# A state-space scan over both channel tiles in one instruction, and no tap products on TensorE

## The chip, the cores and the metric

The kernel runs on one core of a Trainium2 chip. The metric is the device time of one execution in microseconds, the median of several runs. A profile of one execution stands beside it; its own time is given where it is used. The names of the engines are those of the profile: PE is TensorE (PEld its weight loads), DVE is VectorE, ACT is ScalarE, POOL is GpSimd and SP is SyncE.

## The reference

Eight images of 256 channels and 1024 positions pass through a state-space block with an MLP, then through attention and a mixture of experts. The change concerns the state-space block alone:

```python
xz = x @ W_in
xm, z = jnp.split(xz, 2, axis=-1)                # 512 channels each
xp = jnp.pad(xm, ((0, 0), (d_conv - 1, 0), (0, 0)))
xm = sum((xp[:, k:k + L, :] * conv_w[:, k] for k in range(d_conv))) + conv_b   # 4 taps
xm = jax.nn.silu(xm)
dbl = xm @ W_x
dt, Bm, Cm = jnp.split(dbl, [dt_rank, dt_rank + d_state], axis=-1)
dt = jax.nn.softplus(dt @ W_dt + b_dt)
A = -jnp.exp(A_log)

def step(h, inputs):                             # 1024 positions, 16 states a channel
    dt_t, B_t, C_t, x_t = inputs
    dA = jnp.exp(dt_t[..., None] * A)
    h = dA * h + (dt_t * x_t)[..., None] * B_t[:, None, :]
    y = jnp.einsum('bds,bs->bd', h, C_t)
    return (h, y)

y = ys.transpose(1, 0, 2) + xm * D_param
y = y * jax.nn.silu(z)
return y @ W_out
```

For each image, channel and state, `h` is a linear recurrence over the positions: a decay `dA`, an input, and a sum over states of `h` times `C`.

## The kernel before, in words

The work is cut into 16 chunks `i` of 512 positions (`CH`), two for each image; `c = i % NCH` is 0 for an image's first chunk and 1 for its second. The 512 channels lie in four tiles of 128 partitions; two tiles make a half `h`. A chunk has 32 steps (`NSTEP`): 16 states times two halves, numbered on through all chunks as `g`. A step handles one state `s` for one half, that is [128, 2, 512] numbers.

The main loop (L2226 on) writes the steps out one after the other. For step `now` it issues:

- `scan`: the recurrence, on DVE, in place in a tile `hb`. In an image's first chunk the two channel tiles lie one behind the other as 1024 columns and one scan runs over both, because the decay of the second tile's first column is zero and no state is carried in. In the second chunk each channel tile has a scan of its own that begins from its column of `state`. In the first chunk POOL then copies the last column of both tiles to `state`.
- `decay` of step `now + 2`: the exponentials that make `da_all`, on ACT, in one of two buffers. In second chunks the one for the first tile is issued between the two scans.
- `inputs` of step `now + 1`: the product of `xd` with the broadcast row of B, on DVE, into a free `hb`.
- `sums` of `now`: the product with the row of C, on DVE, in place in `hb`; then a DMA issued by POOL adds `hb` to the accumulator `acc` (named `dx` in the profile), which began as D times x. Two accumulators are in use, one for each half, so each such DMA follows the one of two steps before.

`hb` has four slots (`h4`); a fifth is the tile of the weights `w_z`, once they are no longer needed (it appears in the profile as `w_z`). The tiles `t4` (25) hold everything else of this size.

Everything else runs as generators ("streams") beside this loop: `prologue` (projection, the four taps, softplus, for the next chunk), `epilogue` (gate, output projection, MLP), `attention`, `project`, `experts`. `advance()` steps them as long as a small planner, which adds up an estimated cost for each engine, says that their engine is due. The order on each engine's queue is thus fixed when the program is built, and each engine works through its queue in that order. `FRONT[i]` is the step of chunk `i` at which the next chunk's prologue starts, `GATE[i]` that of its gate. `SOFT[i]` lets POOL's DMAs and ACT do two products of the softplus that DVE does otherwise.

The four taps are, as a rule, one ACT operation and three DVE multiply-adds for each channel tile (`conv_parked`, L635; `conv_dve` for the first two chunks). Where `CONV[i]` is 1 (chunks 3, 4 and 13) they are products on PE with diagonal blocks `taps`, 64 matrix products a chunk, which the profile counts as 128:

```python
for r in range(4):
    rows = slice(HD * r, HD * r + HD)
    pe.matmul(
        ps[rows, :], taps[rows, d * KW + t, :], xps[q][rows, t : t + CH],
        start=(t == 0), stop=(t == KW - 1),
    )
```

POOL's queue holds the state copies, all accumulating DMAs (those of the steps; those of softplus into `dt`; those of the epilogue, the projection and the experts' results) and the gathers of expert weights (`g<-eW_d,rows`, `g<-in_eW,rows`), six at a time.

Of the kernel before, what the change touches and what calls it, by code (L numbers as in the profile page):

```python
# [54 lines left out]
def hybrid_kernel(ctx: ExitStack, tc: tile.TileContext, a: dict, out: bass.AP):  # L55
# [95 lines left out]
    w_z = load("w_z", [P, KC, DI], a["W_in"].rearrange("(k p) n -> p k n", p=P)[:, :, DI:])  # L151
# [69 lines left out]
    taps = const.tile([P, ND * KW, HD], F32, name="taps")  # L221
# [50 lines left out]
    FRONT = (7, 13, 4, 4, 1, 14, 10, 1, 13, 1, 10, 6, 1, 5, 10)  # L272
    GATE = (20, 4, 30, 30, 22, 7, 30, 18, 28, 25, 5, 28, 30, 30, 12, 26)
    CONV = (0, 0, 0, 1, 1, 0, 0, 0, 0, 0, 0, 0, 0, 1, 0, 0)
    SOFT = (1, 0, 0, 1, 0, 0, 0, 0, 1, 0, 1, 0, 0, 0, 0, 0)
# [274 lines left out]
    set_up, gates_ready, centered_w = [], [], []  # L550
# [43 lines left out]
    def conv_pe(i, xn, mem):  # L594


        c = i % NCH
        while not set_up:
            yield POLL
        xm, xp, ps, ps2 = [], None, None, None  # L600
        for d in range(ND + 1):
            if d < ND:
                if d % 2 == 0:
                    xm.append((yield from mem.take(f"xm_{i}_{d // 2}")))

                ps2 = yield from banks.take(f"xin_{i}_{d}")
                for k in range(KC):
                    pe.matmul(
                        ps2, w_in[:, k, d * P : (d + 1) * P], xn[:, k, :],
                        start=(k == 0), stop=(k == KC - 1),  # L610
                    )
            if d:
                for t in range(KW):
                    for r in range(4):
                        rows = slice(HD * r, HD * r + HD)
                        pe.matmul(
                            ps[rows, :], taps[rows, (d - 1) * KW + t, :], xp[rows, t : t + CH],
                            start=(t == 0), stop=(t == KW - 1),
                        )
                if c < NCH - 1:  # L620
                    act.copy(conv_tail[:, c + 1, d - 1, :], xp[:, CH:])
            yield
            if d:
                h, q = divmod(d - 1, 2)
                act.activation(xm[h][:, q, :], ps, AF.Identity, bias=V("conv_b", d - 1))
                banks.put(ps)
            if d < ND:
                xp = work_pool.tile([P, KW - 1 + CH], F32, name=f"xp_{i}_{d}", tag="xp", bufs=2)
                act.activation(xp[:, KW - 1 :], ps2, AF.Identity, bias=b_in[:, d : d + 1])
                act.copy(xp[:, : KW - 1], conv_tail[:, c, d, :])  # L630
                ps = ps2
            yield
        return xm

    def conv_parked(i, mem):  # L635
# [5 lines left out]
        for h in range(NHALF):  # L641
# [11 lines left out]
            if CONV[i]:  # L653
                for q in range(2):
                    d = 2 * h + q
                    ps = yield from banks.take(f"cv_{i}_{d}")
                    for t in range(KW):
                        for r in range(4):
                            rows = slice(HD * r, HD * r + HD)
                            pe.matmul(  # L660
                                ps[rows, :], taps[rows, d * KW + t, :], xps[q][rows, t : t + CH],
                                start=(t == 0), stop=(t == KW - 1),
                            )
                    yield
                    act.activation(xm[h][:, q, :], ps, AF.Identity, bias=V("conv_b", d))
                    banks.put(ps)
                continue
# [17 lines left out]
    def prologue(i: int):  # L685
# [23 lines left out]
        def skip_path():  # L709

            for h in range(NHALF):
                dx = me["acc", h] = yield from mem.take(f"dx_{i}_{h}")
                for r in range(2):
                    act.activation(
                        dx[:, r, :], xm[h][:, r, :], AF.Identity, scale=V("D", 2 * h + r)
                    )
# [160 lines left out]

    def load_bc(n):
# [12 lines left out]
    def decay(g, q):  # L891
        i, s, h = place(g)
        da = da_all[:, g % 2, q, :]
# [4 lines left out]
        if skip and g % NSTEP < 2:  # L898
            act.copy(da[:, :1], zero_c)
# [8 lines left out]
    def inputs(g):  # L908
# [11 lines left out]
    def scan(g, q):  # L920

        i, s, h = place(g)
        c = i % NCH
        hb = hbs[g]
        d = 2 * h + q
        done = das.pop((g, q))
        vec.at = max(vec.at, done)
        if c == 0:
            if q:
                both = hb.rearrange("p a t -> p (a t)")  # L930
                vec.tensor_tensor_scan(
                    both, da_all[:, g % 2].rearrange("p a t -> p (a t)"), both, 0.0,
                    ALU.mult, ALU.add,
                )
        else:
            vec.tensor_tensor_scan(
                hb[:, q, :], da_all[:, g % 2, q, :], hb[:, q, :], state[:, s, d : d + 1],
                ALU.mult, ALU.add,
            )
        if q and c < NCH - 1:  # L940
            pool.tensor_copy(state[:, s, 2 * h : 2 * h + 2], hb[:, :, CH - 1])

    def sums(g):
# [14 lines left out]
    def park():  # L958
# [29 lines left out]
        h4.make = lambda nm, k: w_z if k == H4 else make(nm, k)  # L988
# [50 lines left out]
    def epilogue(i: int):  # L1039
# [20 lines left out]
        for h in range(NHALF):  # L1060
            yield me["landed", h]
            if c < NCH - 1:
                vec.tensor_tensor(
                    me["acc", h][:, :, CH - 1], me["dx_end"][:, 0, h], me["dx_end"][:, 1, h],
                    ALU.add,
                )
            vec.tensor_tensor(y[h], me["acc", h], y[h], ALU.mult)
# [1008 lines left out]
    with tc.tile_pool(name="work", bufs=1) as work_pool:  # L2076

        def tagged(tag, n):
            return Slots(
                lambda nm, k: work_pool.tile([P, 2, CH], F32, name=nm, tag=f"{tag}_{k}"), n  # L2080
            )
# [81 lines left out]
        def setup():  # L2163
# [15 lines left out]
            blk = pl.tmp("eye_b", [P, HD], F32)  # L2179
            yield  # L2180
            for r in range(4):
                rows = slice(HD * r, HD * r + HD)
                vec.tensor_copy(blk[rows, :], eye[rows, rows])
            vec.tensor_tensor(
                taps, blk.unsqueeze(1).to_broadcast([P, ND * KW, HD]),
                V("conv_w").unsqueeze(2).to_broadcast([P, ND * KW, HD]), ALU.mult,
# [358 lines left out]
```

## Time and profile before

| | before |
|---|---|
| median of 3 runs | 3393.05 us (3391.55 to 3400.25) |
| the profiled execution's own time | 3395.24 us |
| its span | 3393.4 us |
| mean granted TensorE clock | 0.963 |
| scans of 512 columns (second chunks) | 448 + 64 at 1268 and 1266 ns |
| scans of 1024 columns (first chunks) | 225 + 31 at 2285 and 2282 ns |
| products with B, with C | 512 each, about 1.20 and 1.22 us |
| exponentials of a step's decays, ACT | two, about 0.72 us each |
| state copies, POOL | 225 + 31, 0.18 to 5.5 us, median 1.03 us |
| accumulating DMAs of the steps | 449 + 63, issue 0.89 to 0.94 us, median landing after 7.8 and 6.7 us |
| tap products on PE | 384, 43.4 us busy |
| multiply-adds of the taps, DVE | 156, 741 ns |
| gathers of expert weights, POOL | 64 at 1563 ns and 32 at 1424 ns |

The span is the time from the first to the last instruction of the program; the execution's own time has some 2 us around it. Where two counts are given, the second is that of the slot that bears the name `w_z`. In the tables of stretches each line has the stretch, its length, and for PE, PEld, DVE, ACT and POOL the busy time with the number of instructions, then the granted clock, the DMA engines' busy share, and GB/s. In the views by order of time a line has start, duration, engine, line, operation, output and inputs, shape, and in brackets the idle time before it and what ended it. Nearly all lines of code are L98 or L95, since one helper records every instruction.

### The profile page before, as it was taken

What the parts mean: (1) busy time and instruction counts of PE and PEld (TensorE: products, weight loads), DVE (VectorE), ACT (ScalarE), POOL (GpSimd) and SP (SyncE); (2) the same over time, 40 slices, a digit from 0 to 9 for tenths busy, and PEclk for the clock granted to TensorE, in tenths of its full rate; (3) what the DMA queues carried; (4) which work ended last, traced back from release to release, by engine and by line L of the source; (5) the groups of instructions that cost most, each with busy time, mean ns of one, the idle gap of its engine ahead of it and who ended that gap; (6) DMA issues with size and microseconds to landing.
All of it is one profiled execution on the core that took longest, in us unless ns stands there. A gap on an engine that the chain in (4) does not pass through costs nothing. (4 is left out here: it accounts for less than half of the span.)

```text
span 3393.4 us, 44585 instructions
## 1 busy us (share of the span) xinstructions
PE 3141.3 (93%) x16359; PEld 1387.0 (41%) x16359; DVE 2993.7 (88%) x3140; ACT 2467.8 (73%) x3610; POOL 1104.5 (33%) x1072
## 2 busy tenths in 40 slices
PE   8888988999899999999999899999899989999998
PEld 5444443433343334333444344333443343334343
DVE  6999999899999979899999999999999999962561
ACT  4766756678867887687779777787768868864643
POOL 0242145313432235334353245133542453211010
PEclk9989989999999999999999999999999989999999
DMA  4877899989988898889998999799998998972140
GB/s 138 237 204 189 218 219 219 227 209 232 222 218 228 195 214 202 211 206 217 225 250 190 224 228 216 185 217 219 232 237 201 227 224 186 211 171 71 39 96 23
DMA packets 216134, 668.21 MB, mean 197 GB/s; under 512 B 31200, under 2 KB 42592, under 8 KB 215904
## 3 DMA queue, kind: packets, MB, share of 16 engines
q0 software_dynamic: 106112, 373.88, 56.5%
q1 hardware_dynamic: 109792, 291.38, 25.3%
q8 instruction: 130, 2.13, 0.2%
q14 instruction: 100, 0.82, 0.1%
HBM read 269.20 MB, written 92.93 MB: 107 GB/s over the span
## 5 line engine op out<-in xcount | busy, mean ns | idle before, releaser
L98 ACT ACTIVATE da_all<-dt,vecs 128x512 f32<-128x512 f32 (+1 forms) x1024 | 699.4, 717 | 287.9 <-DVE hb L98 244.8
L95 POOL DMA_DIRECT2D dx<-hb x449 | 397.3, 890 | 1363.5 <-DVE hb L98 960.8
L98 DVE TENSOR_TENSOR hb<-xm,bc 128x1024 f32<-128x1024 f32 x449 | 540.0, 1203 | 22.5 <-issue 19.8
L98 DVE TENSOR_TENSOR_SCAN hb<-da_all,state,hb 128x512 f32<-128x512 f32 x448 | 552.7, 1268 | 4.2 <-ACT da_all L98 4.1
L98 ACT ACTIVATE pt<-sc 128x1024 f32<-128x1024 f32 x512 | 494.6, 1018 | 81.5 <-PE sc L98 70.9
L98 DVE TENSOR_TENSOR hb<-hb,bc 128x1022 f32<-128x1022 f32 (+1 forms) x449 | 546.7, 1218 | 0.0
L98 DVE TENSOR_TENSOR_SCAN hb<-da_all,hb 128x1024 f32<-128x1024 f32 x225 | 514.2, 2285 | 8.3 <-ACT da_all L98 8.3
L98 PE MATMUL warm<-mean_c,zero_c 128*128 128x256 f32 x1182 | 366.0, 433 | 48.9 <-ACT z L98 11.5
L98 POOL COPY state<-hb 128x2 f32<-128x2 f32 x225 | 330.6, 1471 | 206.4 <-DVE hb L98 201.2
L98 PE MATMUL sc<-qk,qk 32*128 32x512 f32 x2048 | 337.7, 647 | 18.2 <-ACT pt L98 17.1
L98 PEld LDWEIGHTS warm<-mean_c,zero_c 128*128 128x128 f32 x1182 | 219.6, 206 | 191.7 <-PE warm L98 73.3
L98 PE MATMUL num<-pt,v 128*32 128x512 f32 x2048 | 279.6, 616 | 13.2 <-DVE ot L98 13.2
L98 PE MATMUL den<-pt,ecb 128*32 128x512 f32 x1792 | 239.0, 604 | 0.0
L98 PE MATMUL re<-he,g 128*128 128x512 f32 x472 | 221.6, 615 | 18.5 <-ACT sz L98 7.8
L98 PE MATMUL facc<-fh,w 128*128 128x512 f32 x512 | 232.8, 601 | 5.9 <-ACT fo L98 2.4
L98 PE MATMUL fh<-x_f,w 128*128 128x512 f32 x480 | 227.1, 604 | 7.2 <-DVE x_f L98 2.5
L98 PE MATMUL he<-xe,g 128*128 128x512 f32 x448 | 219.0, 615 | 5.7 <-issue 3.5
L98 ACT ACT_TABLE_LOAD x159 | 204.0, 1283 | 3.5 <-PEq L2532 0.7
L98 PEld LDWEIGHTS sc<-qk,qk 32*128 32x128 f32 x2048 | 101.0, 185 | 198.3 <-ACT pt L98 80.3
L98 PEld LDWEIGHTS facc<-fh,w 128*128 128x128 f32 x512 | 95.4, 192 | 132.3 <-issue 118.1
L98 PEld LDWEIGHTS re<-he,g 128*128 128x128 f32 x472 | 89.9, 196 | 133.2 <-issue 103.8
L98 PEld LDWEIGHTS fh<-x_f,w 128*128 128x128 f32 x480 | 86.5, 190 | 133.9 <-issue 100.3
(422 smaller groups left out, 4705.4 us busy)
## 6 DMA issues: line engine op xcount, KB each, us to landing
dx<-hb POOLq DMA_DIRECT2D x449, 512.0 KB, 7.8
bc<-bc_d SPq DMA_DIRECT2D x256, 512.0 KB
dx<-w_z POOLq DMA_DIRECT2D x63, 512.0 KB, 6.7
dt<-e POOLq DMA_DIRECT2D x36, 512.0 KB, 9.5
dt<-u POOLq DMA_DIRECT2D x30, 512.0 KB, 11.4
xin_d<-z SPq DMA_DIRECT2D x28, 512.0 KB
sz_d<-z SPq DMA_DIRECT2D x28, 512.0 KB
sz<-sz_d SPq DMA_DIRECT2D x28, 512.0 KB
```

Of the source, the lines that this page charges most:

```text
L95: f(*args, **kw)
L98: return f(*args, **kw)
```

## The change

In second chunks the two channel tiles lie in a row of 1025 columns: 512, one column between, 512. The decay of the middle column is zero from the start of the program on, and its input is the carried state of the second tile, which POOL copies there from `state` when the step's inputs are made. One scan then runs over all 1025 columns: it begins from the first tile's state, is reset in the middle column to the second tile's, and goes on. The accumulating DMA moves the whole row, the middle column with it, which nothing reads. First chunks keep their 1024 columns. All tiles of this size become 1026 columns wide, `w_z` too.

The exponentials of both tiles are issued after the scan, in all chunks. The tap products on PE are gone, with their constants: chunks 3, 4 and 13 compute their taps on DVE as the others do. `FRONT`, `GATE` and `SOFT` have other numbers.

```diff
-    w_z = load("w_z", [P, KC, DI], a["W_in"].rearrange("(k p) n -> p k n", p=P)[:, :, DI:])
+    w_z_all = const.tile([P, 2 * CH + 2], F32, name="w_z")
+    w_z = w_z_all[:, : KC * DI].rearrange("p (k n) -> p k n", k=KC)
+    loads.append((w_z, a["W_in"].rearrange("(k p) n -> p k n", p=P)[:, :, DI:]))
...
-    taps = const.tile([P, ND * KW, HD], F32, name="taps")
...
-    FRONT = (7, 13, 4, 4, 1, 14, 10, 1, 13, 1, 10, 6, 1, 5, 10)
-    GATE = (20, 4, 30, 30, 22, 7, 30, 18, 28, 25, 5, 28, 30, 30, 12, 26)
-    CONV = (0, 0, 0, 1, 1, 0, 0, 0, 0, 0, 0, 0, 0, 1, 0, 0)
-    SOFT = (1, 0, 0, 1, 0, 0, 0, 0, 1, 0, 1, 0, 0, 0, 0, 0)
+    FRONT = (6, 12, 5, 4, 1, 13, 12, 1, 11, 1, 10, 3, 10, 1, 10)
+    GATE = (29, 4, 29, 30, 25, 9, 30, 15, 28, 23, 9, 27, 30, 20, 12, 18)
+    SOFT = (0, 0, 0, 1, 0, 0, 0, 0, 0, 0, 1, 0, 0, 0, 0, 1)
...
-    def conv_pe(i, xn, mem):
...
-            if CONV[i]:
...
-            xm = yield from (conv_pe if CONV[i] else conv_dve)(i, xn, mem)
+            xm = yield from conv_dve(i, xn, mem)
...
+                x, more = xm[h].rearrange("p a t -> p (a t)"), c > 0
+                act.activation(
+                    dx[:, : CH + more], x[:, : CH + more], AF.Identity, scale=V("D", 2 * h)
+                )
+                act.activation(
+                    dx[:, CH + more : 2 * CH + more], x[:, CH:], AF.Identity,
+                    scale=V("D", 2 * h + 1),
+                )
+                dx = halves(i, dx)
...
+    def flat(i, t):
+        return t[:, : 2 * CH + (i % NCH > 0)]
+
+    def halves(i, t):
+        if i % NCH == 0:
+            return t[:, : 2 * CH].rearrange("p (a t) -> p a t", a=2)
+        return t.rearrange("p (a t) -> p a t", a=2)[:, :, :CH]
...
-        da = da_all[:, g % 2, q, :]
+        da = halves(i, da_all[:, g % 2])[:, q, :]
...
-        if skip and g % NSTEP < 2:
-            act.copy(da[:, :1], zero_c)
...
+        if i % NCH:
+            pool.at = max(pool.at, vec.at)
+            pool.tensor_copy(hb[:, CH : CH + 1], state[:, s, 2 * h + 1 : 2 * h + 2])
+            das[g, 2] = pool.at + 0.3
         xd = chunk[i]["xd"][h]
-        vec.tensor_tensor(hb, xd, bc[:, 0, :].unsqueeze(1).to_broadcast([P, 2, CH]), ALU.mult)
+        vec.tensor_tensor(
+            halves(i, hb), xd, bc[:, 0, :].unsqueeze(1).to_broadcast([P, 2, CH]), ALU.mult
+        )
...
-    def scan(g, q):
+    def scan(g):
...
+        for q in range(3):
+            vec.at = max(vec.at, das.pop((g, q), 0.0))
+        vec.tensor_tensor_scan(
+            hb, flat(i, da_all[:, g % 2]), hb,
+            state[:, s, 2 * h : 2 * h + 1] if i % NCH else 0.0, ALU.mult, ALU.add,
+        )
+        if i % NCH < NCH - 1:
+            pool.tensor_copy(
+                state[:, s, 2 * h : 2 * h + 2], halves(i, hbs[g])[:, :, CH - 1]
+            )
...
-        y = hb[:, :, :n]
+        y = halves(i, hb)[:, :, :n]
...
-        me["landed", h] = pool.dma_start(out=me["acc", h], in_=hb, accum_op=ALU.add)
+        me["landed", h] = pool.dma_start(out=flat(i, me["acc", h]), in_=flat(i, hb), accum_op=ALU.add)
...
-        da_all = work_pool.tile([P, 2, 2, CH], F32, name="da_all", tag="da")
+        da_all = work_pool.tile([P, 2, 2 * CH + 2], F32, name="da_all", tag="da")
+        pool.memset(da_all[:, :, CH : CH + 1], 0.0)
...
-            for q in range(2):
-                scan(now, q)
-                advance()
-                if now + 2 < nsteps and (q or i % NCH):
-                    for r in range(0 if i % NCH == 0 else q, q + 1):
-                        decay(now + 2, r)
+            scan(now)
+            advance()
+            if now + 2 < nsteps:
+                for q in range(2):
+                    decay(now + 2, q)
```

More of the change, by code (lines that the diff above doesn't have):

```diff
@@ L549, in hybrid_kernel @@
     capacity = float(math.ceil(B * L * 1.25 / E))
-    set_up, gates_ready, centered_w = [], [], []
+    gates_ready, centered_w = [], []
     open_sums = []
@@ L592, in conv_dve @@
         return xm
-    def conv_pe(i, xn, mem):
[L597 to L633, printed above, removed]
     def conv_parked(i, mem):
@@ L652, in conv_parked @@
             yield landed
-            if CONV[i]:
-                for q in range(2):
[L655 to L667, printed above, removed]
             for q in range(2):
@@ L712, in skip_path @@
                 dx = me["acc", h] = yield from mem.take(f"dx_{i}_{h}")
[L713 to L716, printed above, removed]
+                x, more = xm[h].rearrange("p a t -> p (a t)"), c > 0
[7 more added lines that the diff above has]
+                dx = halves(i, dx)
                 if c < NCH - 1:
@@ L914, in inputs @@
         vec.at = max(vec.at, landed)
+        if i % NCH:
+            pool.at = max(pool.at, vec.at)
+            pool.tensor_copy(hb[:, CH : CH + 1], state[:, s, 2 * h + 1 : 2 * h + 2])
+            das[g, 2] = pool.at + 0.3
         xd = chunk[i]["xd"][h]
-        vec.tensor_tensor(hb, xd, bc[:, 0, :].unsqueeze(1).to_broadcast([P, 2, CH]), ALU.mult)
+        vec.tensor_tensor(
+            halves(i, hb), xd, bc[:, 0, :].unsqueeze(1).to_broadcast([P, 2, CH]), ALU.mult
+        )
         if s == NS - 1:
             t4.put(xd)
-    def scan(g, q):
+    def scan(g):
         i, s, h = place(g)
[L923 to L938, printed above, removed]
-            )
-        if q and c < NCH - 1:
-            pool.tensor_copy(state[:, s, 2 * h : 2 * h + 2], hb[:, :, CH - 1])
+        hb = flat(i, hbs[g])
+        for q in range(3):
[7 more added lines that the diff above has]
+                state[:, s, 2 * h : 2 * h + 2], halves(i, hbs[g])[:, :, CH - 1]
+            )
     def sums(g):
@@ L987, in park @@
         make = h4.make
-        h4.make = lambda nm, k: w_z if k == H4 else make(nm, k)
+        h4.make = lambda nm, k: w_z_all if k == H4 else make(nm, k)
         h4.free.append((model.t, H4))
@@ L1063, in epilogue @@
                 vec.tensor_tensor(
-                    me["acc", h][:, :, CH - 1], me["dx_end"][:, 0, h], me["dx_end"][:, 1, h],
+                    halves(i, me["acc", h])[:, :, CH - 1], me["dx_end"][:, 0, h], me["dx_end"][:, 1, h],
                     ALU.add,
                 )
-            vec.tensor_tensor(y[h], me["acc", h], y[h], ALU.mult)
+            vec.tensor_tensor(y[h], halves(i, me["acc", h]), y[h], ALU.mult)
             t4.put(me["acc", h])
@@ L2078, in tagged, with make @@
         def tagged(tag, n):
-            return Slots(
-                lambda nm, k: work_pool.tile([P, 2, CH], F32, name=nm, tag=f"{tag}_{k}"), n
-            )
+            def make(nm, k):
+                t = work_pool.tile([P, 2 * CH + 2], F32, name=nm, tag=f"{tag}_{k}")
+                if nm[:2] in ("dx", "hb"):
+                    return t
+                return t[:, : 2 * CH].rearrange("p (a t) -> p a t", a=2)
+            return Slots(make, n)
         t4, h4, pt4 = tagged("t4", T4), tagged("h4", H4), tagged("pt", PT)
-        da_all = work_pool.tile([P, 2, 2, CH], F32, name="da_all", tag="da")
+        da_all = work_pool.tile([P, 2, 2 * CH + 2], F32, name="da_all", tag="da")
+        pool.memset(da_all[:, :, CH : CH + 1], 0.0)
         for b in range(B):
@@ L2178, in setup @@
             make_identity(nc, eye)
-            blk = pl.tmp("eye_b", [P, HD], F32)
             yield
[L2181 to L2186, printed above, removed]
-            )
             vec.tensor_tensor(pick3, eye[:, 0:4], eye[:, 4:8], ALU.add)
             vec.tensor_tensor(pick3, pick3, eye[:, 8:12], ALU.add)
-            set_up.append(True)
             yield
@@ L2252, in hybrid_kernel @@
                     idle(0.5)
-            for q in range(2):
-                scan(now, q)
-                advance()
-                if now + 2 < nsteps and (q or i % NCH):
-                    for r in range(0 if i % NCH == 0 else q, q + 1):
-                        decay(now + 2, r)
+            scan(now)
[3 more added lines that the diff above has]
+                    decay(now + 2, q)
             if now == 0:
```

## The prediction

> **What bounds the kernel now.** I read the page first, then a table of stretches by chunk, then groups by shape, then the order of time on DVE and POOL. I call a chunk odd when it is the second of its image, and a step one half of the channels for one of the 16 states.
>
> The busy times and the slices of the page:
>
> ```profile
> PE 3141.3 (93%) x16359; PEld 1387.0 (41%) x16359; DVE 2993.7 (88%) x3140; ACT 2467.8 (73%) x3610; POOL 1104.5 (33%) x1072
> ...
> DVE  6999999899999979899999999999999999962561
> ...
> DMA  4877899989988898889998999799998998972140
> ```
>
> DVE is full until slice 35 (its last step ends at 3014 us) and then no more. The last 380 us are attention and experts of the last image, with PE busy for 356 of them. PE's share misleads: 433.4 us of it are filler multiplications ("warm" 366.0, and 67.4 into an open sum). So DVE sets the pace of 16 chunks, and a fixed tail follows. Four stretches (length, then PE, PEld, DVE, ACT, POOL busy, clock, DMA share, GB/s): two odd chunks, an even one, the tail's first half.
>
> ```profile
> 659.00:830.30 171.30, 161.86 (x972) 61.16 (x970) 167.21 (x159) 137.03 (x197) 32.70 (x38) 0.98 0.91 219
> ...
> 1773.50:1948.80 175.30, 158.56 (x808) 62.42 (x812) 170.35 (x163) 145.90 (x201) 47.49 (x48) 0.95 0.91 210
> 1948.80:2130.30 181.50, 176.11 (x954) 79.59 (x946) 177.62 (x184) 131.72 (x195) 91.11 (x84) 0.97 0.93 221
> ...
> 3013.30:3200.00 186.70, 183.85 (x918) 79.93 (x916) 67.07 (x130) 99.86 (x128) 18.29 (x19) 1.00 0.29 73
> ```
>
> DVE works for 97 to 98% of these chunks (91 and 89% in chunks 2 and 5). The DMA engines stand at 0.91 beside it, and POOL is little used in odd chunks.
>
> DVE in order of time, an odd chunk's step:
>
> ```profile
> 699.53 2.45 DVE L98 TENSOR_TENSOR_SCAN hb<-da_all,state,hb 128x512 f32<-128x512 f32 x2
> 701.90 1.20 DVE L98 TENSOR_TENSOR hb<-xm,bc 128x1024 f32<-128x1024 f32 x1
> 703.02 1.22 DVE L98 TENSOR_TENSOR hb<-hb,bc 128x1024 f32<-128x1024 f32 x1
> 704.15 2.45 DVE L98 TENSOR_TENSOR_SCAN hb<-da_all,state,hb 128x512 f32<-128x512 f32 x2
> ```
>
> and an even chunk's:
>
> ```profile
> 499.61 2.28 DVE L98 TENSOR_TENSOR_SCAN hb<-da_all,hb 128x1024 f32<-128x1024 f32 x1
> 501.81 1.20 DVE L98 TENSOR_TENSOR hb<-xm,bc 128x1024 f32<-128x1024 f32 x1
> 502.93 1.21 DVE L98 TENSOR_TENSOR hb<-hb,bc 128x1022 f32<-128x1022 f32 x1
> 504.06 2.28 DVE L98 TENSOR_TENSOR_SCAN hb<-da_all,hb 128x1024 f32<-128x1024 f32 x1
> ```
>
> Neighbours overlap by some 0.08 us, so starts count, not durations: from scan to product 2.37 us for the pair (699.53 to 701.90), 2.20 for one scan (499.61 to 501.81). A step is 4.62 or 4.45 us.
>
> POOL in order of time, its copies of the state in an even chunk, and its gathers of expert weights in odd chunk 9:
>
> ```profile
> 497.90 3.97 POOL L98 COPY state<-hb 128x2 f32<-128x2 f32 x1
> 501.81 0.85 POOL L95 DMA_DIRECT2D dx<-hb  x1
> 502.35 3.97 POOL L98 COPY state<-hb 128x2 f32<-128x2 f32 x1
> ```
>
> ```profile
> 1826.11 1.95 POOL L95 DMA_INDIRECT g<-eW_d,rows  x1 [0.30 <-issue]
> 1828.36 2.02 POOL L95 DMA_INDIRECT g<-eW_d,rows  x1 [0.30 <-issue]
> 1830.67 2.00 POOL L95 DMA_INDIRECT g<-eW_d,rows  x1 [0.30 <-issue]
> 1832.97 1.41 POOL L95 DMA_INDIRECT g<-eW_d,rows  x1 [0.30 <-issue]
> 1834.39 1.94 POOL L95 DMA_DIRECT2D dx<-hb  x2
> ```
>
> A copy of two columns can take 4 us, since it ends only where a scan ends (501.87 beside 501.89). Six gathers hold POOL for 12.6 us (1821.75 to 1834.38); the steps' accumulates wait behind them.
>
> [...] The trace has 2.37 - 2.20 = 0.17 us. [...] Today's rows of 512 KB over 128 partitions are 4096 B; the new ones have 4100. No accumulate of such a row is in this trace.
>
> **The change part by part.** Sums are against the profiled execution: 3395.24 us, of which the span is 3393.4. The median of the runs shown is 3393.05, 2.2 us less.
>
> *One scan for two.* 8 odd chunks x 32 steps = 256 steps, each 2.37 - 2.20 = 0.17 us shorter on DVE; the extra column is 2.28 us / 1024 = 2 ns. **-43.5 us**, all on the pacing engine. The durations alone (2 x 1.268 - 2.285 = 0.25 us) would promise 64.
>
> *Tap products move from PE to DVE* for chunks 3, 4 and 13. PE loses 43.4 us, which is worth little beside 433 us of filler. DVE gains 12 multiply-adds per chunk, 36 in all: those of the other chunks have 741 ns and start 0.67 us apart (six span 4.04 us at 2525.96). 36 x 0.67 = **+24 us** on the pacing engine. Its cover would be waits of DVE that shrink; inside most chunks DVE waits only for 2 to 3%. Bounds: +8 (PE was the tighter one in those places) to +27 (at 741 ns). I take 24. The taps' setup (one 0.69 us product and four small copies) goes: about -1.5 us, early, beside waits; counted as nothing.
>
> *One POOL copy per odd step, and a new wait.* The carried state is copied into column 512 of the row, and the scan waits for it. In POOL's queue the copy for step g+1 stands behind the accumulate of step g-1, which waits for that step's output product, and behind whatever else was queued: gathers, other accumulates, an accumulate's wait for the previous landing in the same tile (8.5 us at 2986). Behind the copy stand step g's accumulate, which needs a later product anyway; behind the scan stand all DVE work and the exponentials that rewrite its decays on ACT. In the steady case it fits: the accumulate starts 0.3 us after the product and takes 0.86, so POOL is free 1.15 us into a step of 4.45, the copy ends with the running scan at 2.2, and 2.2 us are spare. If POOL is late by more than about 3.1 us (4.45 less 1.15 and 0.2 for an unblocked copy), DVE stands.
>
> How late is POOL today, when nobody minds? From the order of time, for all 256 odd steps: start of the accumulate minus end of its product. It exceeds 1.2 us in 70 steps and 3.1 us in 33. The excess over 3.1 sums to 73 us, 50 of it within two steps of gathers (7 of the 14 blocks of the loop fall in odd chunks), 23 elsewhere, mostly chunk 15. Not all 73 is paid: a step that waits lets POOL catch up for the next, and gathers run in 0.95 us instead of 1.95 when DVE is idle, as the tail shows. [...] And the start steps (FRONT, GATE) are other numbers and the planner counts the copy, so some gathers may move to even chunks. Bounds: 5 us (all moved) to 105 us[...]. I take **+45**.
>
> *Rows of 1025 accumulated whole.* 256 accumulates of 4100 B per partition. At the same rate 0.1% more: nothing. If a row costs a second packet, the bound is what a packet costs now (56.5% of 16 x 3393 us over 106112 packets = 289 ns)[...]. I take 0, with up to +40 where a row breaks into equal parts and the DMA share of 0.91 rises.
>
> *The rest.* Exponentials of both tiles now follow the whole scan, with nearly two steps before they are needed, as in even chunks today. Two 1-column ACT copies per even chunk go. D products get one column more. SOFT lists three working chunks before and after (chunk 0 does not use it). Nothing.
>
> Sum on DVE: -43.5 + 24 + 45 = +25.5 us. The tail gives some back: its PE work includes the experts of the seventh image, which move forward while DVE stands. I pass on 0.8: **+20 us**, 3415 for the profiled execution, **3413 us** for the median.
>
> **The rivals.**
> *A. The copy hides, faster.* Its place is the odd step; it decides if late POOL work costs less than 20 us in all. For it: POOL is busy only 18 to 30% of odd chunks, and start steps are redrawn. Against: seven gather blocks of 10 to 16 us, which follow attention, not the chunk. With 10 us of stall and conv at half its price: -43.5 + 12 + 10 = -21.5, 3371 us.
> *B. No change.* Stall about 20 us, or the tail takes up the rest: 3393 us within 10 (0.3%, what a measurement of this kernel can tell from none). For it: PE is at 98% in the tail's first half.
> *C. Transfers lose.* 4100-byte rows break, or landings slip with DMA at 0.91; with 105 us of stall, or 65 and 40 for the transfers: -43.5 + 24 + 105 = +85, less the tail's fifth: 3461 us. Against: nothing in the trace hints at a break.
>
> **How the numbers follow.** Forecast (slower by 10 to 45 us) 0.44; A 0.32; B 0.14; C 0.10. Faster by over 0.3%: 0.32; within: 0.14; slower: 0.54. The forecast's own range is 3403 to 3438. With cases of both signs the range is 3355 (A with hardly a stall and conv at +8) to 3455.
>
> **What would show it.** A scan of 1025 columns x256 at about 2.29 us with idle time before it released by POOL's copy, 40 us or more in sum and longest (5 to 12 us) behind gathers; 192 xm multiply-adds; no tap products; accumulates' landings near the median of 7.8 us. A is right if that idle time is under 20 us; C if landings or software packets grow. I am wrong at the root if DVE falls clearly below 95% in odd chunks for another reason than POOL.

## The result and the profile after

The changed kernel takes 3446.34 us (median of 4 runs, 3438.60 to 3453.26) against 3396.65 us (4 runs, 3391.55 to 3401.48) for the kernel before on the same chip: ratio 1.0134, 95% interval 1.0093 to 1.0175 (the two medians alone would give 1.0146). It is slower. The profiled execution took 3443.63 us with a span of 3441.8, 48.4 us more than the span before.

Where the time lies, from the starts of the first scans of the chunks: the eight first chunks of the images grew from 1524.2 to 1569.4 us (+45.2), the eight second chunks, in which the scan was changed, went from 1423.5 to 1422.5 (-1.0), the part before the first scan +0.3, the tail (what follows the last product with C) from 378.9 to 382.7 (+3.8). That the second chunks stayed as long is a balance: on DVE their scans take 28.5 us less (609.0 to 580.5, from start to next start without idle time), and DVE stands idle before them 36.0 us more (4.2 to 40.2). Of the growth of the first chunks 14.0 us lie in chunk 0 alone, while chunk 1 became 8.8 us shorter.

The busy times and slices of the changed kernel's page:

```profile
PE 3145.6 (91%) x16005; PEld 1387.8 (40%) x16005; DVE 3001.1 (87%) x2915; ACT 2457.2 (71%) x3594; POOL 1196.3 (35%) x1329
...
DVE  6979999899999979999999999999999999962561
...
DMA  4958999889999988799998999799989998872140
```

The page hardly differs. DVE has 225 instructions fewer and is 7 us busier, POOL 92 us busier, PE the same (its tap products went, the filler `warm` grew from 366.0 to 380.5 us). The stretches that answer to those shown before (chunks 3, 9 and 10, and the tail's first half; length, then PE, PEld, DVE, ACT, POOL busy, clock, DMA share, GB/s):

```profile
679.90:861.20 181.30, 170.84 (x1050) 66.10 (x1048) 178.54 (x150) 150.40 (x214) 64.19 (x71) 1.00 0.90 219
1801.60:1974.00 172.40, 159.49 (x809) 62.74 (x807) 165.57 (x128) 138.83 (x191) 76.61 (x79) 0.96 0.93 211
1974.00:2165.00 191.00, 176.99 (x926) 79.69 (x926) 181.05 (x188) 134.35 (x200) 79.68 (x86) 0.91 0.92 214
3059.10:3245.80 186.70, 183.95 (x927) 79.71 (x924) 65.88 (x129) 100.88 (x128) 18.15 (x19) 1.00 0.27 71
```

POOL's busy time in chunk 3 doubled from 32.7 to 64.2 us: the copies. The tail is as long as it was. A step of a second chunk, DVE in order of time (start, duration):

```profile
693.78 2.34 DVE L98 TENSOR_TENSOR_SCAN hb<-da_all,state,hb 128x1025 f32<-128x1025 f32 x1
696.04 1.20 DVE L98 TENSOR_TENSOR hb<-xm,bc 128x1024 f32<-128x1024 f32 x1
697.16 1.21 DVE L98 TENSOR_TENSOR hb<-hb,bc 128x1024 f32<-128x1024 f32 x1
698.29 2.34 DVE L98 TENSOR_TENSOR_SCAN hb<-da_all,state,hb 128x1025 f32<-128x1025 f32 x1
```

From scan to product it is 2.26 us where the pair took 2.37, and the step takes 4.51 where it was 4.62. The gain is 0.11 us, not 0.17. A step of a first chunk, first DVE, then POOL:

```profile
898.59 2.29 DVE L98 TENSOR_TENSOR_SCAN hb<-da_all,hb 128x1024 f32<-128x1024 f32 x1
900.79 1.20 DVE L98 TENSOR_TENSOR hb<-xm,bc 128x1024 f32<-128x1024 f32 x1
902.07 1.22 DVE L98 TENSOR_TENSOR hb<-hb,bc 128x1022 f32<-128x1022 f32 x1
903.21 2.28 DVE L98 TENSOR_TENSOR_SCAN hb<-da_all,hb 128x1024 f32<-128x1024 f32 x1
```

```profile
900.93 1.10 POOL L98 COPY state<-hb 128x2 f32<-128x2 f32 x1 [1.12 <-DVE hb L98]
```

This step grew from 4.45 to 4.62 us though no instruction of it is longer. The product with C starts 1.28 us after the product with B, where it was 1.12. The copy of the state ends at 902.03, just after the product with B (901.99), and the product with C begins at 902.07: it now waits for that copy. No idle time is printed in brackets, because most of the loss is the overlap of neighbours that is gone; only the starts show it. (Copies of 4 us, as in the prediction, are the smaller part. In the kernel before 38 of 256 take 3.9 us or more, and 37 of these end within 0.06 us of the end of a scan; the median of all is 1.03 us, about the length of a product.)

And a late copy in chunk 11, POOL in order of time, then DVE:

```profile
2246.96 0.86 POOL L95 DMA_DIRECT2D dx<-hb  x1 [1.40 <-issue]
2248.12 1.44 POOL L95 DMA_INDIRECT g<-in_eW,rows  x1 [0.30 <-issue]
...
2255.88 0.94 POOL L95 DMA_INDIRECT g<-eW_d,rows  x1 [0.30 <-issue]
2256.83 0.19 POOL L98 COPY hb<-state 128x1 f32<-128x1 f32 x1
```

```profile
2249.73 1.22 DVE L98 TENSOR_TENSOR hb<-hb,bc 128x1024 f32<-128x1024 f32 x1
2257.05 2.35 DVE L98 TENSOR_TENSOR_SCAN hb<-da_all,state,hb 128x1025 f32<-128x1025 f32 x1 [6.11 <-issue]
```

Six gathers stand in POOL's queue ahead of a copy of one column that takes 0.19 us, and DVE stands idle for 6.11 us until that copy has ended at 2257.02. (In this trace the 1319 copies, DMA issues and memsets of POOL start, kind by kind, in the program's order; so do 2698 operations of DVE and 3369 of ACT.) The groups by shape (busy, mean ns of one | idle time before it, and what ended it):

```profile
L98 DVE TENSOR_TENSOR_SCAN hb<-da_all,state,hb 128x1025 f32<-128x1025 f32 x224 | 526.0, 2348 | 29.5 <-issue 9.7 <-ACT da_all L98 8.8 <-POOL hb L98 8.7
L98 DVE TENSOR_TENSOR_SCAN hb<-da_all,hb 128x1024 f32<-128x1024 f32 x224 | 511.5, 2283 | 1.8 <-ACT da_all L98 1.7
L98 DVE TENSOR_TENSOR hb<-hb,bc 128x1022 f32<-128x1022 f32 x224 | 273.3, 1220 | 26.3 <-POOL state L98 16.6
L98 DVE SCALAR_TENSOR_TENSOR xm<-xp,vecs,xm 128x512 f32<-128x512 f32 x192 | 130.0, 744 | 14.8 <-ACT xm L98 14.8
```

Two numbers here were not foreseen: 2348 ns for the scan, where 1024 columns without a carried state take 2283, and the 26.3 us of idle time before products with C in first chunks (30.5 with the slot `w_z`), a wait that the kernel before did not have. Of the 30.5 us, 19.0 are five long waits for POOL's copy of the state, of up to 8.34 us; the longest two stand behind gathers, as the late column copies do. The rest is 0.08 us in each of nearly 150 places.

### The profile page after: what moved, and what is told of

The parts are those of the page before. It is cut to its first block, busy times and chain, and to the rows that moved or that the text cites. A ratio compares the mean times of both kernels' runs of the same rounds, so it can differ in the third digit from the quotient of the medians.

```text
span 3441.8 us, 43740 instructions
## 1 busy us (share of the span) xinstructions
PE 3145.6 (91%) x16005; PEld 1387.8 (40%) x16005; DVE 3001.1 (87%) x2915; ACT 2457.2 (71%) x3594; POOL 1196.3 (35%) x1329
## 3 DMA queue, kind: packets, MB, share of 16 engines
q0 software_dynamic: 106112, 374.01, 56.2%
## 4 chain that ended last, share of the span: by engine, by line
PE 19%; DVE 17%; issue 8%; DMA 6%; ACT 5%; POOL 4%; DVEq 0%; POOLq 0%; ACTq 0%
DVE hb L98 10%; DMA dx<-hb 3%; PE num L98 2%; DVE w_z L98 2%; PE he L98 2%; PE sc L98 2%; DMA dx<-w_z 2%; PE re L98 2%; DVE xm L98 1%; POOL state L98 1%; PE halves L98 1%; PE fh L98 1%; PE facc L98 1%; PE warm L98 1%; POOL dx L95 1%
## 5 line engine op out<-in xcount | busy, mean ns | idle before, releaser
L98 ACT ACTIVATE da_all<-dt,vecs 128x512 f32<-128x512 f32 (+1 forms) x1024 | 680.8, 715 | 316.8 <-DVE hb L98 276.1
L95 POOL DMA_DIRECT2D dx<-hb x448 | 387.6, 866 | 1299.7 <-DVE hb L98 806.1
L98 DVE TENSOR_TENSOR hb<-hb,bc 128x1022 f32<-128x1022 f32 (+1 forms) x448 | 546.3, 1219 | 26.3 <-POOL state L98 16.6
L98 DVE TENSOR_TENSOR_SCAN hb<-da_all,state,hb 128x1025 f32<-128x1025 f32 x224 | 526.0, 2348 | 29.5 <-issue 9.7
L98 DVE TENSOR_TENSOR_SCAN hb<-da_all,hb 128x1024 f32<-128x1024 f32 x224 | 511.5, 2283 | 1.8 <-ACT da_all L98 1.7
L98 PE MATMUL warm<-mean_c,zero_c 128*128 128x256 f32 x1170 | 380.5, 444 | 49.6 <-ACT dt L98 13.3
L98 POOL COPY hb<-state 128x1 f32<-128x1 f32 x224 | 294.7, 1316 | 0.0
L98 POOL COPY state<-hb 128x2 f32<-128x2 f32 x224 | 195.4, 872 | 276.4 <-DVE hb L98 254.6
```

The source lines that it names most:

```text
L95: f(*args, **kw)
L98: return f(*args, **kw)
```

## The experiments

In six of the runs the order of all other instructions on every engine's queue was held as in the changed kernel (runs 1, 2 and 9 to 12), by charging the planner the same costs. In run 4 it was held as in the kernel before. In the others the planner ordered anew. Executions of one kernel lie up to 30 us apart (the changed kernel's from 3438.60 to 3453.26, run 2's from 3410.02 to 3436.04), so a difference of two spans, of one execution each, can be off by some 10 us; where it matters, the difference of the ratios stands beside it. Idle times in the table and the text are summed over DVE's instructions in order of time: each instruction's start less the latest end before it. "Start to next start" leaves out the idle time before the next one. "C" is the product with C in first chunks, "scan" the scans of second chunks, each with the slot `w_z`.

| run | median us | ratio to before (95%) | span | first chunks | second chunks | idle before C | idle before scan |
|---|---|---|---|---|---|---|---|
| before | | 1 | 3393.4 | 1524.2 | 1423.5 | 0.0 | 4.2 |
| after | 3446.34 | 1.0134 (1.0093 to 1.0175) | 3441.8 | 1569.4 | 1422.5 | 30.5 | 40.2 |
| 1 tiles of first chunks | 3433.58 | 1.0077 (1.0048 to 1.0106) | 3427.6 | 1545.1 | 1429.8 | 11.1 | 40.8 |
| 2 no column copy | 3426.93 | 1.0067 (1.0054 to 1.0080) | 3417.8 | 1568.5 | 1402.1 | 30.9 | 6.7 |
| 3 before, no PE taps | 3478.33 | 1.020 (1.017 to 1.023) | 3482.8 | 1543.6 | 1490.7 | 0.0 | 4.5 |
| 5 after, old steps | 3546.09 | 1.0422 (1.0405 to 1.0440) | 3540.9 | 1563.7 | 1519.8 | 38.2 | 59.6 |
| 6 as 3, new steps | 3461.66 | 1.0167 (1.0148 to 1.0186) | 3461.0 | 1528.1 | 1464.6 | 0.0 | 4.7 |
| 7 early copy, new order | 3458.34 | 1.0172 (1.0145 to 1.0199) | 3452.5 | 1555.9 | 1436.8 | 3.9 | 32.6 |
| 8 copy on ACT | 3562.25 | 1.0460 (1.0438 to 1.0482) | 3566.5 | 1534.3 | 1605.3 | 18.8 | 194.3 |
| 9 1024 straight | 3398.06 | 0.9978 (0.9959 to 0.9997) | 3396.1 | 1540.0 | 1404.8 | 0.0 | 9.0 |
| 10 taps left out | 3446.31 | 1.0107 (1.0072 to 1.0143) | 3443.3 | 1570.3 | 1426.3 | 34.5 | 41.4 |
| 11 two scans | 3441.22 | 1.0104 (1.0081 to 1.0126) | 3441.3 | 1573.3 | 1419.7 | 34.2 | 2.7 |
| 12 early copy, same order | 3405.29 | 1.0012 (0.9997 to 1.0027) | 3401.6 | 1544.5 | 1408.3 | 7.4 | 17.3 |

The kernel before measured 3396.65 to 3404.07 us in the four sets of runs, so ratios are compared, not medians.

**1. Separate tile forms in first chunks.** My theory after reading the trace: the wait before the product with C exists only because the program's dependence tracking no longer sees that columns 0 to 510 of each half and the copied columns 511 are disjoint, now that both are views cut out of one flat row.

```diff
...
+                if nm[:2] == "hb" and n // NSTEP % NCH == 0 or nm[:2] == "dx" and n % NCH == 0:
+                    return work_pool.tile([P, 2, CH], F32, name=nm, tag=f"{tag}_{k}")
                 t = work_pool.tile([P, 2 * CH + 2], F32, name=nm, tag=f"{tag}_{k}")
...
```

> The changed kernel, but in first chunks hb and dx are tiles of shape [128, 2, 512] again (the slot that is w_z stays flat); queues and their order are the same as in the changed kernel. Theory 1 (the product with C waits in first chunks for POOL's state copy only because the flat rows hide that their columns are disjoint): the wait of hb<-hb,bc for POOL goes from 26 us to nothing but for the w_z slot (about 4 us left), the products with B overlap again, and the kernel gets 30 to 45 us faster than the changed one, 3400 to 3416 us. Rival (the time went into first chunks because the start steps are other ones): the wait goes, but the time stays within 10 us of 3446.

The groups of this run:

```profile
L98 DVE TENSOR_TENSOR hb<-hb,bc 128x1022 f32<-128x1022 f32 x224 | 271.9, 1214 | 0.0
...
L98 DVE TENSOR_TENSOR w_z<-w_z,bc 128x1022 f32<-128x1022 f32 x32 | 39.1, 1221 | 11.1 <-POOL state L98 9.3
```

With the same instructions in the same order the wait is gone for all 224 tiles of the four slots and left for the slot `w_z`, which stayed flat. So the form of the tiles makes the wait; that it does so by way of the dependence tracking is the plainest reading, and no run tests it apart. The gain is smaller than I expected: first chunks became 24.3 us shorter, 7.3 came back in second chunks, 2.9 before the first scan, and the span fell by 14.2 us. By the ratios it is 19 us, give or take 17.

**2. No copy of the column.** POOL's copy is left out (fixed `hb` tiles, their middle column set to zero once; the second tile's recurrence then begins from zero).

```diff
-            pool.tensor_copy(hb[:, CH : CH + 1], state[:, s, 2 * h + 1 : 2 * h + 2])
+            model.do(pool, 1.2)
...
```

> The changed kernel without POOL's copy of the carried state into column 512 (leaves out the carried state of every second channel tile in second chunks); the hb slots are fixed tiles. Theory (POOL's copy comes late behind gathers, accumulates and landings): idle time of DVE before the 1025-column scans falls from about 40 us to below 10, the kernel gets 25 to 35 us faster than the changed one, about 3415 us. Rival (the scans wait for something else, such as ACT's exponentials): idle time before them stays above 25 us and the time within 10 us of 3446.

Idle before scans fell by 33.5 us, the second chunks by 20.4 and the span by 24.0: some 13 us came back as other waits (21.8 to 35.2 us before other instructions of second chunks). The wait behaved as the theory said, the time less so. The column copy costs 20 to 24 us (23 by the ratios).

**3. The kernel before without tap products on PE.** `CONV` is all zero, nothing else.

```diff
-    CONV = (0, 0, 0, 1, 1, 0, 0, 0, 0, 0, 0, 0, 0, 1, 0, 0)
+    CONV = (0,) * 16
```

> The kernel before with no tap products on PE in any chunk, nothing else changed. Theory (36 more multiply-adds lie on the pacing engine): 24 us slower than before, 3420 us. Rival (PE was as tight in these chunks, so its 43 us come back): within 10 us of before.

It costs 2.0%, some 70 us; neither figure was met. DVE's taps take 24.0 us more, as expected (from start to next start, 95.2 to 119.2). The rest is idle time before instructions other than scans and products with B and C: 98.4 to 176.1 us. The order on all queues had changed, and with it what waits for what, so this run does not price the taps.

**4. The start value of a scan.** In the kernel before, the scan of first chunks takes its start value from a column of zeros in SBUF instead of the constant 0.

```diff
-                    both, da_all[:, g % 2].rearrange("p a t -> p (a t)"), both, 0.0,
+                    both, da_all[:, g % 2].rearrange("p a t -> p (a t)"), both, zero_c,
```

> The kernel before, but the scan of 1024 columns in first chunks takes its start value 0 from a column in SBUF and not as a number. Theory (a start value read from SBUF costs a fixed time, and that is why 1025 columns took 2.348 us): the 1024-column scan goes from 2.285 to about 2.345 us, and the kernel gets about 15 us slower than before. Rival (the odd count or the row's place in memory costs it): 2.285 us, and the time unchanged.

```profile
L98 DVE TENSOR_TENSOR_SCAN hb<-da_all,zero_c,hb 128x1024 f32<-128x1024 f32 x225 | 527.6, 2345 | 7.5 <-ACT da_all L98 7.4
```

2345 ns against 2285: a start value read from SBUF costs 0.06 us. The whole took 3414.86 us, in a single execution.

**5 and 6. The start steps.** Run 5 is the changed kernel with the old `FRONT`, `GATE` and `SOFT`; run 6 is run 3 with the new ones.

```diff
-    FRONT = (6, 12, 5, 4, 1, 13, 12, 1, 11, 1, 10, 3, 10, 1, 10)
+    FRONT = (7, 13, 4, 4, 1, 14, 10, 1, 13, 1, 10, 6, 1, 5, 10)
...
```

> The changed kernel with FRONT, GATE and SOFT of the kernel before. Theory 1 (the new start steps are a repair for the taps: without them the waits of the run without tap products come back): DVE's idle time before other instructions than scans and products with B or C rises from 90 to 120 us or more, and the median from 3446 to 3465-3495 us. Rival (the new start steps themselves are what the change lost): the median falls below 3436 us.

> The kernel before with CONV all zero (no tap products on PE), as in the earlier run, but with the new FRONT, GATE and SOFT. Theory 1 (the taps cost their 24 us on DVE, and the new steps take away what the queues lost on top): 3415-3440 us, DVE conv in even and odd chunks as in the earlier run (63.7 and 55.5 us), idle before other instructions back near 100-120 us in sum (176 in the earlier run). Rival (the new steps fit only the chunks with one scan; moving the taps costs more than their DVE time in any order): 3455-3480 us.

Run 5 is far slower than either figure, 99 us in the span over the changed kernel, with the same work but for the softplus products that `SOFT` moves: the direction of theory 1, not its size. In run 6 the rival was right: the new steps don't make up for the moved taps in a kernel with two scans. The new steps are worth 2.9% in the changed kernel and 0.3% in this one, and so neither run gives the price of the taps alone. That needed run 10.

**7 and 12. The copy earlier in POOL's queue.** Both have the tiles of run 1. The tile of step `now + 2` is taken, and its column copied, before the accumulate of `now` is issued. In run 7 the planner is told of it and orders anew; in run 12 it is not, and all else keeps its order.

```diff
+            n = now + 2
+            if n < nsteps and n // NSTEP % NCH and h4.free:
+                reserve(n)
             sums(now)
...
```

> The changed kernel with separate tile forms in first chunks, as in the first experiment, and the copy of the carried state issued one step earlier, ahead of the accumulate and of the gathers that stood before it in POOL's queue. Theory 1 (the scan waits because the copy stands late in POOL's queue): idle time before scans of 1025 columns falls from 40 us to under 15 us and the median to 3405-3420 us. Rival (the copy is late [...]wherever it stands, or another wait takes its place): idle before these scans stays over 25 us, or idle before other instructions rises by as much; median 3425-3438 us.

> Separate tile forms in first chunks, as in the first experiment, and the copy of the carried state one step earlier in POOL's queue, but this time with the order of all else on every queue as in the changed kernel (the run before let the order change). Theory 1 (the copy's place in POOL's queue makes the wait): idle before scans of 1025 columns falls from 40 to under 20 us, median 3413-3423 us (3433.6 in the first experiment). Rival (the copy waits for the accumulate that frees its tile[...] and is as late one step earlier): idle before these scans over 28 us, median 3430 us or more.

Run 12, groups:

```profile
L98 DVE TENSOR_TENSOR_SCAN hb<-da_all,state,hb 128x1025 f32<-128x1025 f32 x224 | 526.2, 2349 | 16.5 <-ACT da_all L98 9.4 <-POOL hb L878 7.0
...
L878 POOL COPY hb<-state 128x1 f32<-128x1 f32 x224 | 291.0, 1301 | 134.9 <-DMA dx<-hb 134.9
```

In run 12 the copies now wait 134.9 us for tiles to come free, and almost none of it reaches DVE: 7.0 us of idle time before scans is left to POOL, the rest of the 17.3 to ACT's exponentials. The copies are as long as ever (1301 ns, 1316 in the changed kernel), so it is the place in the queue that cost, not the length of the copy. Run 12 spans 26.0 us less than run 1 (22 by the ratios) and measures like the kernel before (1.0012). Run 7 met its rival's figures for the waits. It does nearly the same work and spans 50.9 us more than run 12; idle before scans is 32.6 us there, half of it now ended by ACT's exponentials, and other waits of second chunks rose to 56.6 us (30.6 in run 12). That is what a new order can cost by itself.

**8. The copy on ACT.** The tiles of run 1, and ACT copies the column where POOL did.

```diff
-            pool.tensor_copy(hb[:, CH : CH + 1], state[:, s, 2 * h + 1 : 2 * h + 2])
+            act.copy(hb[:, CH : CH + 1], state[:, s, 2 * h + 1 : 2 * h + 2])
...
```

> As the one before in its tiles (separate forms in first chunks), but the copy of the carried state is made by ACT, at the place in the program where POOL made it. ACT pays about 0.19 us for each of 256 copies, 49 us in sum, beside DVE. Theory 1 (POOL's queue is the cause): idle before scans of 1025 columns falls under 15 us, median 3405-3420 us. Rival (ACT is then late, because its copy waits in order for a free slot and the exponentials stand behind it): idle before these scans, released by ACT, stays over 30 us, median 3430 us or more.

```profile
L98 DVE TENSOR_TENSOR_SCAN hb<-da_all,state,hb 128x1025 f32<-128x1025 f32 x220 | 516.8, 2349 | 156.1 <-ACT hb L98 155.8
```

The rival was right, and more so: here too the small operation is late by the queue in which it stands. The order was also made anew, so the whole loss is not the copy's. It is no remedy.

**9. All overhead of the merge away.** Second chunks scan 1024 columns straight through; no middle column, no copy, [128,2,512] tiles everywhere (the recurrence of the second tile is not begun anew).

```diff
-        return t[:, : 2 * CH + (i % NCH > 0)]
+        return t.rearrange("p a t -> p (a t)")
...
```

> The changed kernel with all overhead of the merged scan taken away and its order on every queue kept: [128,2,512] tiles everywhere, in second chunks one scan over 1024 columns straight through, no middle column, no copy of the carried state (the second tile's recurrence is not begun anew: that part is left out). Theory 1 (flat tiles cost 13 us and the column copy 20 us, the rest of the loss is taps and order): 3408-3420 us, idle before scans of second chunks under 8 us and before products with C of first chunks under 2 us. Rival A (the 4100-byte rows cost something in the transfers too): under 3405 us. Rival B (waits elsewhere take back what is freed): over 3424 us.

The span is 45.7 us less than the changed kernel's, and the time is that of the kernel before less 0.2%. So the overheads of the row are about as large as the whole loss; the gain of the scan, which this run keeps, and the cost of the moved taps and new steps about offset each other. Runs 1 and 2 account for 38.2 of the 45.7 us (14.2 + 24.0), and run 1 left 11.1 us of waits in the slot `w_z`, more than the 7.5 that remain. So the transfers need no share in it, though theory 1's figure was missed and rival A's (under 3405) was met. By the ratios the run gains 53 us over the changed kernel, and 11 remain.

**10. The taps left out.** The 36 multiply-adds of chunks 3, 4 and 13 are left out, with the planner charged for them.

```diff
+                    if i in (3, 4, 13):
+                        model.do(vec, vec_cost("scalar_tensor_tensor", y))
+                        continue
                     vec.scalar_tensor_tensor(
```

> The changed kernel without the 36 multiply-adds of the taps of chunks 3, 4 and 13 on DVE (left out altogether), order on every queue kept. Theory 1 (DVE pays them in full): 24 us less than the changed kernel in the span (3441.8 to about 3418), median near 3422 us. Rival (waits of DVE on PE and ACT in these chunks take up most): at most 10 us less, median 3436 us or more.

DVE loses 24 us of work and the span gains nothing (3443.3 against 3441.8). By the ratios it is 9 us, but the intervals are too wide to tell that from 0 or from 24. The trace is clearer: in chunks 2, 3 and 12, in which these multiply-adds stood, DVE is busy 22.6 us less and the three together are 3.4 us shorter. Chunk 2, in which the taps of chunk 3 are computed, before (at 484.00), after (at 489.60) and in run 10, as stretches:

```profile
484.00:659.10 175.10, 159.02 (x719) 76.18 (x717) 158.60 (x118) 114.83 (x168) 91.42 (x72) 0.94 0.92 223
```

```profile
489.60:679.90 190.30, 168.40 (x786) 75.68 (x787) 171.83 (x138) 133.00 (x192) 59.70 (x74) 0.93 0.87 210
```

```profile
497.10:687.10 190.00, 168.26 (x786) 75.41 (x787) 164.30 (x126) 132.72 (x192) 58.37 (x74) 0.94 0.87 211
```

DVE's busy time falls by 7.5 us and the chunk by 0.3. Two instructions of DVE in that chunk, after and in run 10, with the wait before them:

```profile
560.90 1.22 DVE L98 SCALAR_TENSOR_TENSOR xe<-mu_a,xe 128x1024 f32<-128x1024 f32 x1 [1.83 <-PE mu_a L98]
...
641.85 1.22 DVE L98 SCALAR_TENSOR_TENSOR xe<-mu_a,xe 128x1024 f32<-128x1024 f32 x1 [11.48 <-PE mu_a L98]
```

```profile
567.63 1.22 DVE L98 SCALAR_TENSOR_TENSOR xe<-mu_a,xe 128x1024 f32<-128x1024 f32 x1 [6.76 <-PE mu_a L98]
...
649.04 1.23 DVE L98 SCALAR_TENSOR_TENSOR xe<-mu_a,xe 128x1024 f32<-128x1024 f32 x1 [10.93 <-PE mu_a L98]
```

DVE arrives earlier and waits longer for PE's mean: 1.83 became 6.76 us at the first, and the second stayed long. The kernel before has no such wait in its chunk 2. The rival was right.

**11. Two scans again.** Run 2, with a scan for each channel tile.

```diff
+            for q in range(2):
+                y = halves(i, hbs[g])[:, q, :]
+                nc.vector.tensor_tensor_scan(
+                    y, halves(i, da_all[:, g % 2])[:, q, :], y,
+                    state[:, s, 2 * h + q : 2 * h + q + 1], ALU.mult, ALU.add,
+                )
...
```

> As the run without column copy (fixed hb tiles, middle column set to zero once), but in second chunks each channel tile has its own scan of 512 columns again, one behind the other; order on every queue otherwise kept. It measures what one scan for two is worth. Theory 1 (0.17 us less 0.06 us for the start value that is read from SBUF): 256 x 0.11 = 28 us more than that run (3426.9, ratio 1.0067): 3455 us, ratio about 1.015. Prediction's figure: 43.5 us more, 3470 us, ratio 1.0195. Rival (DVE's other waits hide part): under 3440 us.

```profile
697.99 2.45 DVE L893 TENSOR_TENSOR_SCAN hb<-da_all,state,hb 128x512 f32<-128x512 f32 x2
700.36 1.20 DVE L98 TENSOR_TENSOR hb<-xm,bc 128x1024 f32<-128x1024 f32 x1
```

The pair has its 2.37 us again, against 2.26 (703.23 - 700.97 in run 2). On DVE the scans take 27.2 us more than in run 2 (607.8 against 580.6, start to next start). The span is 23.5 us longer than run 2's, the second chunks 17.7, and the ratio 0.0037, or 13 us, which is near the rival's figure. One scan for two is worth 13 to 24 us of time, not 43.5.

## Why the prediction was right, and where it was not

The forecast was 3413 us and slower, with 3403 to 3438 as its own range and 3355 to 3455 over all cases. It is 3446: slower, above the forecast's own range and inside the wide one. The cause that was named, a late copy on POOL, is there and costs 20 to 24 us. It does not make the sign alone. Without it the kernel is still slower than before (run 2: 1.0067, interval 1.0054 to 1.0080), and the copy and the scan as measured would nearly cancel (-4 to +11 us). What makes the kernel clearly slower is a term that was put at nothing, the tiles of first chunks, and what the moved taps and the new start steps cost together. The right sign is thus in part luck: the gain of the scan was put 20 to 30 us too high and the price of the copy 21 to 25 us too high, and these two errors cancel.

*One scan for two, -43.5.* The mechanism was right, the size not: 27 to 29 us on DVE (609.0 to 580.5 between the two kernels), of which 13 to 24 reached the time. The step took 2.20 us for one scan from the first chunks, where the start value is a constant; in second chunks it is read from SBUF, which costs 0.06 us (run 4), 15 us over 256 scans. The prediction saw both forms side by side and did not ask in what else they differ. The 0.17 us held the start value for free: with it, 0.11 us (2.37 less 2.26) is what one instruction less is worth here.

*Taps to DVE, +24.* As DVE work exactly right: 192 multiply-adds of 744 ns, 24 us. As time it looks wrong with the order held: leaving them out again gained nothing in the span and 3.4 us in the three chunks (run 10; its ratio, 9 us lower, decides nothing by itself). "Inside most chunks DVE waits only for 2 to 3%" holds for chunk 3, but chunk 2, where the first of the three sets of taps is computed, stood at 91% by the prediction's own reading; there DVE ends up waiting for PE, and its multiply-adds lie in front of that wait. The bound of +8 that the prediction gave was the better value.

*The copy and its wait, +45.* Right in kind, half the size in time. Idle time before the scans of second chunks is 40.2 us, of it some 30 ended by the copy and some 10 by exponentials: between the 40 that the forecast asked for and the 20 of rival A. It is longest behind gathers (6.1 us twice, 3.55 twice), as the prediction said of place and cause, and taking the copy out gains 20 to 24 us. The lateness of POOL in the old trace (73 us beyond the slack) was a fair bound and no estimate: a wait once paid lets POOL catch up (the prediction's reasoning, not measured apart), and the 39 gathers that ran beside an idle DVE in the changed kernel took 0.94 to 0.96 us, against a median of 1.06 us for the 65 during which DVE was busy over half the time. What the bound of 105 us has beyond these 73 is an estimate of the prediction alone. Idle time itself was not the price either: with 33.5 us less of it the span fell by 24.0.

*Rows of 4100 bytes, 0.* Right. The software queue moved 106112 packets before and after, 373.88 and 374.01 MB; the +40 for rows that break was an estimate of the prediction alone. In run 12 both lengths are landed in the same execution (output and input, count, size, median us from issue to landing):

```profile
dx<-hb POOLq DMA_DIRECT2D x224, 512.5 KB, 7.4
dx<-hb POOLq DMA_DIRECT2D x224, 512.0 KB, 7.5
```

*The rest, nothing.* This is the step whose mechanism failed. "First chunks keep their 1024 columns" was true of the arithmetic and not of the tiles: they became views of a flat row, and the product with C, which had run beside POOL's copy of the state, had to wait for it. That costs 14 us with the slot `w_z` left as it is, and up to 22 with it (45.7 of run 9 less 24.0 of run 2); by the ratios 19 and 30. It is why the first chunks lost 24 (run 1) to 29 (run 9) of their 45 us; the rest of the 45 is not the tiles'. The diff showed it (`halves`, `flat`), and the trace before showed copies of the state beside running products, whose cover should have been asked for.

*The tail.* It gave nothing back (+3.8 us), where a fifth of the loss was credited to it.

The terms as measured, in the span: +24.0 for the copy, about +14 to +22 for the flat tiles, -13 to -24 for the scan, together +14 to +33 of the +48.4. By the ratios they are +23, +19 to +30 and -13, together +29 to +40 of 46. What remains, 6 to 34 us, is the taps' move and the new start steps.

Part of it shows in the chunks whose streams compute the moved taps: chunks 2, 3 and 12 are 29.7 us longer after, 26.6 in run 9 and 26.3 in run 10. Since run 10 has none of the taps' multiply-adds, that isn't DVE's work on them; in chunk 2 it shows as waits for PE's means. But not all of it is loss, because the new start steps also move work between chunks: with no multiply-adds of taps in chunk 2 in either, DVE is busy there 158.6 us before and 164.3 in run 10, and chunks 4 and 5 are 9.9 us shorter after than before. One growth goes clearly with the steps: chunk 0 takes 247 to 258 us in the ten profiles with the new steps and 235 to 240 in the four with the old ones (before, runs 3, 4 and 5). Chunk 1 takes back 8.8 of these us in the changed kernel. How much of the whole remainder is the new start steps and how much the absence of PE's products could not be told apart: the kernels that changed one without the other were ordered anew and came out 1.7 to 2.9% longer than the ones they were made from (runs 3, 5 and 6). This stays open.

No version was found that beats the kernel before. The nearest, run 12, equals it. The taps on PE beside the wide rows, and a form of its own for the slot `w_z` in first chunks, were not run.

## What to carry to other kernels

When a tile changes its shape, look at every instruction that touches another part of it: a view cut from a flat row can bring a wait between two operations that share no element (30.5 us of idle time here), and the profile may show it only as starts that no longer overlap (1.28 us from start to start here instead of 1.12). A tiny operation that a pacing engine must wait for costs what stands before it in its queue, not what it takes; issue it as early as its tile is free (22 to 26 us less here, for moving one copy). And test a part with the order of everything else held: in a program whose order is planned by costs, telling the planner of one moved copy or not made 51 us, more than any part of this change was measured to be worth.

## What the runs showed of the hardware that was not expected

- A scan that reads its start value from SBUF takes 0.06 us longer than one that starts from a constant: 2345 and 2346 ns (runs 4 and 9) against 2283 to 2286 for 1024 columns.
- A row of 4100 bytes per partition is accumulated by the same number of software packets as one of 4096 (106112 before and after) and lands as soon (7.4 and 7.5 us in run 12).
- A product that starts right behind another begins about 0.08 us before that one's end (697.16 beside 697.24 in the changed kernel); a wait that ends just then takes this away without any idle time being shown, 13 us in sum here (products with B of first chunks, start to next start: 288.4 to 301.3 us).
